# Wide attention: an earlier first norm, SyncE for the first transfers, maxima spread over the batches, and halves swapped by ScalarE

## The chip, the cores and the metric

The kernel runs on one core of one Trainium2 chip. Time is device microseconds from start to end of one launch. A core has five engines with a queue of instructions each: TensorE (PE; its weight loads are shown as PEld), VectorE (DVE), ScalarE (ACT), GpSimd (POOL) and SyncE (SP, which only starts transfers). ScalarE, SyncE and POOL can issue DMAs. An engine works through its queue in order; engines wait for each other through semaphores, which the Tile framework places from the data that instructions share.

## What is computed

x has 8 batches of 512 rows of 128. Two sublayers follow one another, each as x + layernorm(f(layernorm(x))):

```
x = x + ln(attention(ln(x)))      # one head of width 128, rope, causal; q, k, v and output weights 128x128
x = x + ln(ffn(ln(x)))            # ffn(x) is itself two steps:
    h = rmsnorm(x, g1) @ w_down                     # 128 -> 64
    a = x + attention16(h @ wq, h @ wk, h @ wv) @ w_up   # 16 heads of width 4, rope, causal
    t = rmsnorm(a, g2)
    f = a + sum over the 2 best of 8 experts of gate * (silu(t @ w1[e]) * (t @ w3[e])) @ w2[e]
ln(x) = (x - mean) / sqrt(var + 1e-5);   rope: (even, odd) -> (even*cos - odd*sin, even*sin + odd*cos)
```

In the wide attention "even" and "odd" are the first and the second 64 of the 128 columns.

## The kernel before

All of x, the running result (`h_all`) and all weights stay in SBUF. The work has three stages.

**Wide attention** (class `Wide`, driven by `wide_attention`). One batch is four row tiles of 128. Per batch: statistics of x (`stats_x`, VectorE and POOL), normalised rows on ScalarE (`norm`, L297), four transposes on TensorE and one copy (`turn`), projections to q and k with the rope (`project`), the scores with a causal mask added by a matmul (`scores`, L343 and L344), the maximum of each row on VectorE (L349) and the exponential on ScalarE (L351, which also yields the row sums), transposes of the probabilities (`turn_probs`, L367) and their copies to SBUF, the values (`values`, with `wvo`, the product of value and output weights), the weighted sum (`weigh`, L380), and later the closing: norm of the result (`norm_result`, `add_result`), its sum with x (`add`) and the statistics of that sum (`norm_sum`). The loop is a software pipeline written out by hand: in the round of batch b, batch b+1 is normalised and turned, b is projected and scored, b-1 has its probabilities turned and weighed, and b-2 is closed. Each round has four steps, at whose ends the generator yields.

For the rope the weights of q and k lie in SBUF twice, as they are and with their halves exchanged (`wqk`, six loads). `project` is called twice per batch; each call makes two 128x512 matmuls, multiplies the pair by the cosine and sine tables in one VectorE operation of 1024 columns (L316), and adds the two halves on POOL (L318).

**Head attention** (`Unit`, `period`). A unit is four of the 16 heads of one batch; there are 32. `ffn_front` makes q and k of a batch, splits them into three bf16 parts and writes them to DRAM (L552); `load_rows` reads them back in another layout (L560); both run on POOL's queue. For each unit, `rowwise` and `highest` (L600, L615) find the maximum of each row, in six pieces; `lower` and `turn_m` put these maxima into rows of q, with six small SyncE loads (L641), and then `columnwise`, `weights` and `weigh` (L656, L679, L686) make the transposed scores, their exponentials and the weighted sums. `period(n)` has seven steps; it finds maxima for unit n+2 while it works on unit n. So periods -2 and -1 hold nothing but maxima of units 0 and 1 and the turning of the first.

**Experts** (`experts`, L849 to L874), batch by batch.

What runs beside what is written in the driving loops: at each yield of the wide attention one step is taken from a list of tasks (`setup`: weight preparation and fixed rows; `first`: the front of batch 0; `fronts`: that of batch 1; `then`: periods -2 and -1). In the periods, `aside` takes a step from the fronts of later batches or from the backs of earlier ones. Inside `tc.manual_schedule()` the order on each engine is the order of the program text. The loads ahead of it are outside.

PSUM has eight banks of 512 columns of float32: three tiles of two banks ("wide") and two single banks ("bank") in the first stage, which in the second become one single bank and one for the weighted sums ("po").

Of the kernel before, what the change touches and what calls it, by code (L numbers as in the profile page):

```python
# [22 lines left out]
def kernel(  # L23
# [58 lines left out]
    for b in range(B):  # L82
        nc.sync.dma_start(
            out=x_all[:, b * NT : (b + 1) * NT, :],
            in_=x[b].rearrange("(t p) d -> p t d", p=P),
        )


    wqk = const.tile([P, 2, 2, D], F32, name="wqk")
    for i, w in enumerate((a_wq, a_wk)):  # L90
        nc.scalar.dma_start(out=wqk[:, i, 0, :], in_=w[0])
        nc.scalar.dma_start(out=wqk[:, i, 1, 0 : D // 2], in_=w[0][:, D // 2 : D])
        nc.scalar.dma_start(out=wqk[:, i, 1, D // 2 : D], in_=w[0][:, 0 : D // 2])
    ropea = const.tile([P, 2, T], F32, name="ropea")
    nc.scalar.dma_start(out=ropea, in_=rope_a)
# [5 lines left out]
    wdown = const.tile([P, L], F32, name="wdown")  # L101
    nc.gpsimd.dma_start(out=wdown, in_=w_down)
    wqkv = const.tile([L, 3, L], F32, name="wqkv")
    for i, w in enumerate((f_wq, f_wk, f_wv)):
        nc.gpsimd.dma_start(out=wqkv[:, i, :], in_=w)
    wup = const.tile([L, D], F32, name="wup")
    nc.gpsimd.dma_start(out=wup, in_=w_up)
    wr = const.tile([P, E], F32, name="wr")
    nc.gpsimd.dma_start(out=wr, in_=router_w)
    g1c = const.tile([P, 1], F32, name="g1c")  # L110
    nc.gpsimd.dma_start(out=g1c, in_=g1.rearrange("(p o) -> p o", o=1))
    g2c = const.tile([P, 1], F32, name="g2c")
    nc.gpsimd.dma_start(out=g2c, in_=g2.rearrange("(p o) -> p o", o=1))
    ropef = const.tile([P, NT, 2, HD], F32, name="ropef")
    nc.gpsimd.dma_start(out=ropef, in_=rope_f.rearrange("(t p) s d -> p t s d", p=P))
# [3 lines left out]
    for s in range(2):  # L119
# [10 lines left out]
    ident_bf = const.tile([P, P], BF16, name="ident_bf")  # L130
    nc.vector.tensor_copy(ident_bf, ident)

    mask_a = const.tile([P, P], BF16, name="mask_a")
    nc.gpsimd.memset(mask_a, 0.0)
    nc.gpsimd.affine_select(
        out=mask_a,
        in_=mask_a,
        compare_op=ALU.is_ge,
        fill=NEG_BF,
        base=0,  # L140
        pattern=[[-1, P]],
        channel_multiplier=1,
    )

    def half_masks(name, sign):


        m = const.tile([P, 2, P], BF16, name=name)
        nc.gpsimd.memset(m, 0.0)
        for i in range(2):  # L150
            for h in range(2):
                at = m[i * HR : (i + 1) * HR, h, :]
                nc.gpsimd.affine_select(
                    out=at,
                    in_=at,
                    compare_op=ALU.is_ge,
                    fill=NEG_BF,
                    base=sign * HR * h,
                    pattern=[[-sign, P]],
                    channel_multiplier=sign,  # L160
                )
        return m

    mask_q = half_masks("mask_q", -1)
    mask_k = half_masks("mask_k", 1)

    order = const.tile([P, E], F32, name="order")
    for e in range(E):
        nc.gpsimd.memset(order[:, e : e + 1], float(E - e))
# [47 lines left out]
    half = const.tile([P, 2 * GT], F32, name="half")  # L217
    nc.gpsimd.memset(half, -0.5)

# [38 lines left out]

    wvo = const.tile([P, D], F32, name="wvo")

    def fuse_projections():
        ps = bank("wvo_ps")
        nc.tensor.transpose(ps[:, :P], wv, ident)
        wvT = work.tile([P, D], F32, tag="sq", name="wvT", bufs=1)
        nc.scalar.copy(wvT, ps[:, :P])
        ps = bank("wvo_ps2")
        nc.tensor.matmul(ps[:, :P], wvT, wo, start=True, stop=True)
        nc.scalar.copy(wvo, ps[:, :P])
# [9 lines left out]
    def stats_x(batches):  # L278
        st = ln_stats(x_all, batches[0] * NT, "x", len(batches) * NT)
        for i, b in enumerate(batches):  # L280
            x_stats[b] = st[0][:, i * NT : (i + 1) * NT, :], st[1][:, i * NT : (i + 1) * NT]

    class Wide:
# [7 lines left out]
        def norm(self):  # L291
            b = self.b
            mv, rstd = x_stats.pop(b)
            shift = minus_product(mv[:, :, 0], rstd, "shift_x", f"shift_x_{b}")
# [15 lines left out]
        def project(self, i):  # L310
            b = self.b
            pq = wide(f"pq_{b}_{i}")
            for s in range(2):
                nc.tensor.matmul(pq[:, s, :], wqk[:, i, s, :], self.xnT, start=True, stop=True)
            two = deep.tile([P, 2, T], F32, tag="pk", name=f"two_{b}_{i}", bufs=5)
            nc.vector.tensor_tensor(two, pq, ropea, ALU.mult)  # L316
            r = work.tile([P, T], F32, tag=f"roped{i}", name=f"roped_{b}_{i}", bufs=1)
            nc.gpsimd.tensor_tensor(r, two[:, 0, :], two[:, 1, :], ALU.add)  # L318
            self.roped.append(r)
# [40 lines left out]
        def turn_probs(self, t):  # L360
            b = self.b
            n, at = (t + 1) * P, t * (t + 1) // 2 * P
            if t == 0:
                self.pT = work.tile([P, 10 * P], F32, tag="pT", name=f"pT_{b}", bufs=1)
            ps = bank(f"pT_ps_{b}_{t}")
            for j in range(t + 1):
                nc.tensor.transpose(  # L367
                    ps[:, j * P : (j + 1) * P], self.probs[t][:, j * P : (j + 1) * P], ident
                )
            if t < 2:  # L370
                nc.vector.tensor_copy(self.pT[:, at : at + n], ps[:, :n])
            else:
                nc.scalar.copy(self.pT[:, at : at + n], ps[:, :n])
# [22 lines left out]
        def norm_result(self):  # L396
            self.r = ln_stats(h_all, self.b * NT, "r")
            self.shift = minus_product(
                self.r[0][:, :, 0], self.r[1], "shift_r", f"shift_r_{self.b}"
            )  # L400

        def add_result(self):
            n0 = self.b * NT
            for t in range(NT):
                nc.scalar.activation(
                    h_all[:, n0 + t, :],
                    h_all[:, n0 + t, :],
                    AF.Identity,
                    bias=self.shift[:, t : t + 1],
                    scale=self.r[1][:, t : t + 1],  # L410
                )

        def add(self):
            nc.gpsimd.tensor_tensor(
                x_all[:, self.tiles, :], x_all[:, self.tiles, :], h_all[:, self.tiles, :], ALU.add
            )

        def norm_sum(self):
# [13 lines left out]
            h_scale[b] = kept  # L432

# [68 lines left out]

    def ffn_front(b):
# [43 lines left out]
        for r in range(3):  # L547
            for dst, src in (
# [3 lines left out]
                nc.gpsimd.dma_start(out=dst.rearrange("a d h t -> (d h) a t"), in_=src)  # L552
# [3 lines left out]
    def load_rows(b):  # L556
        for rows, src in zip((q_rows[b % 2], k_rows[b % 2]), made[b][0:2]):
            halves = src.rearrange("r a d (p i) t -> i (r a d) p t", i=2)
            for i in range(2):
                nc.gpsimd.dma_start(out=rows[i * HR : i * HR + S9], in_=halves[i])  # L560
# [414 lines left out]

    def wide_attention():
        batches = [Wide(b) for b in range(B)]
        for g in ([0], [1]):
            stats_x(g)
        batches[0].norm()  # L980
        batches[0].turn()
        fuse_projections()
        for b in range(B + 2):
            yield b
            u = batches[b] if b < B else None
            nxt = batches[b + 1] if b + 1 < B else None
            v = batches[b - 1] if 0 <= b - 1 < B else None
            w = batches[b - 2] if 0 <= b - 2 < B else None
            if nxt:
                nxt.norm()  # L990
            if w:
                w.norm_result()
            if u:
                u.project(0)
            if v:
                v.turn_probs(0)
                v.turn_probs(1)
            if u:
                u.project(1)
            yield b  # L1000
# [3 lines left out]
            if w:  # L1004
                w.add_result()
# [5 lines left out]
            yield b  # L1011
            if v:
                v.weigh()
            if b + 2 < B:
                stats_x([b + 2])
# [4 lines left out]
            yield b  # L1020
            if u:
                u.scores(1)
            yield b
# [5 lines left out]

    with tc.manual_schedule():  # L1030
        steps = wide_attention()
        setup = [prepare(), fill()]
        first = [front_and_rows(0)]
        then = [period(-2), period(-1)]
        fronts.append(front_and_rows(1))
        banks(ctx, wide=3)
        with ExitStack() as stage:
            banks(stage, bank=2)
            for b in steps:
                if b > B:  # L1040
                    break
                if b < 3:
                    step(setup)
                elif b < 6:
                    step(first)
                elif b < 7:
                    step(fronts)
                else:
                    step(fronts)
                    step(then)  # L1050
            while step(then):
                step(fronts)
    banks(ctx, bank=1, po=1)
    with tc.manual_schedule():
        for n in range(N + 1):
            for _ in period(n):
                next(steps, None)
                aside()
        for _ in experts(0):
# [79 lines left out]
```

## Time and profile before

| | us |
|---|---|
| median of 3 runs (821.34 to 822.37) | 822.21 |
| the profiled execution | 826.83 |
| its span, from first to last instruction | 825.0 |
| TensorE busy | 734.2 (89%) |
| VectorE busy | 479.0 (58%) |
| ScalarE busy | 334.9 (41%) |
| POOL busy | 310.2 (38%) |

The span divides at three marks in the trace: the first score matmul (25.14), the first weighing of the head attention (174.52) and the first expert (about 477). In the profile's lines, "out<-in" names what an instruction writes and reads, "x4" stands for four of them merged into one line, and brackets tell how long the engine sat idle before and what ended the wait. A row of digits gives tenths in 40 slices of the span, of about 20.6 us each. PEclk is the clock that TensorE was granted, as a share of full speed.

### The profile page before, as it was taken

The numbers are of one execution on the slowest core, as the hardware profiler recorded it, in microseconds if no ns is written. First come the engines' busy times: TensorE is split into PE (matmuls) and PEld (weight loads), VectorE is DVE, ScalarE is ACT, GpSimd is POOL, SyncE is SP. The second block draws the span as 40 slices with busy tenths as digits, with TensorE's granted clock in tenths as the row PEclk, the third lists the DMA queues.
The fourth block names the chain that finished last, engine by engine and source line by source line (L and its number), as shares of the span: only waits on it lengthen the run. The fifth ranks groups of instructions, "written<-read, shape, count | busy, mean of one in ns | idle before, by whom it ended". The sixth has DMA issues, their size and how long they took to land. (4 is left out here: it accounts for less than half of the span.)

```text
span 825.0 us, 15055 instructions
## 1 busy us (share of the span) xinstructions
PE 734.2 (89%) x5886; PEld 436.8 (53%) x5886; DVE 479.0 (58%) x1069; ACT 334.9 (41%) x532; POOL 310.2 (38%) x638
## 2 busy tenths in 40 slices
PE   2989687479999999989889899999999999999994
PEld 1646454334444445444444455666666666666663
DVE  1565557657766767686866035745454545454543
ACT  2454343155666656565656623222222222222220
POOL 5476876636666757676725130101010101010101
PEclk9999799669999999999999999999999999999998
DMA  9002120402221304040400000000000000000000
GB/s 287 20 14 71 58 58 1 116 2 61 60 72 49 101 19 118 3 117 4 118 3 3 2 1 0 14 1 14 0 14 1 14 0 14 1 14 0 14 1 13
DMA packets 25770, 30.37 MB, mean 37 GB/s; under 512 B 6372, under 2 KB 20932, under 8 KB 25700
## 3 DMA queue, kind: packets, MB, share of 16 engines
q0 software_dynamic: 6944, 19.03, 8.9%
q1 hardware_dynamic: 17460, 9.48, 3.9%
q8 instruction: 46, 0.75, 0.4%
q10 hardware_dynamic: 1296, 0.92, 0.4%
q14 instruction: 24, 0.20, 0.1%
HBM read 15.73 MB, written 11.53 MB: 33 GB/s over the span
## 5 line engine op out<-in xcount | busy, mean ns | idle before, releaser
L615 DVE TENSOR_REDUCE nm<-sm 128x2 f32<-128x1024 f32 (+2 forms) x192 | 194.3, 1044 | 45.0 <-PE sm L583 27.8
L679 ACT ACTIVATE pk<-sT 128x1024 f32<-128x1024 f32 x160 | 160.8, 1024 | 76.7 <-PE sT L583 76.6
L857 ACT ACTIVATE sil<-ph 128x512 f32<-128x512 f32 x128 | 76.4, 597 | 251.8 <-PE ph L849 230.3
L858 DVE TENSOR_TENSOR hid<-sil,ph 128x512 f32<-128x512 f32 x128 | 87.3, 687 | 124.2 <-ACT sil L857 124.2
L865 PEld LDWEIGHTS py<-w2s,hid 128*128 128x128 f32 x1024 | 124.2, 192 | 31.9 <-issue 27.4
L849 PE MATMUL ph<-tT_all,w1s 128*128 128x512 f32 x256 | 132.5, 600 | 0.0
L849 PE MATMUL ph<-tT_all,w3s 128*128 128x512 f32 x256 | 131.6, 596 | 0.0
L865 PE MATMUL py<-w2s,hid 128*128 128x128 f32 x1024 | 124.8, 275 | 1.9 <-DVE h_all L874 1.2
L224 POOL TENSOR_TENSOR root_o<-ve_o,half 128x4 f32<-128x4 f32 x8 | 8.2, 1020 | 310.0 <-DVE ve_o L241 310.0
L686 PE MATMUL po<-pk,vpad 128*32 128x512 f32 (+3 forms) x1024 | 98.5, 452 | 0.0
L874 DVE SCALAR_TENSOR_TENSOR h_all<-py,gate_all,h_all 128x128 f32<-128x128 f32 x256 | 72.0, 344 | 30.3 <-PE py L865 30.3
L600 PE MATMUL sm<-k_rows,q_rows 61*128 61x256 bf16 (+3 forms) x512 | 72.7, 310 | 12.3 <-DVE nm L615 7.3
L849 PEld LDWEIGHTS ph<-tT_all,w3s 128*128 128x128 f32 x256 | 49.1, 192 | 62.0 <-issue 62.0
L656 PE MATMUL sT<-q_rows,k_rows 64*128 64x384 bf16 (+3 forms) x512 | 65.4, 303 | 14.6 <-DVE nm L615 8.4
L849 PEld LDWEIGHTS ph<-tT_all,w1s 128*128 128x128 f32 x256 | 44.3, 193 | 31.9 <-issue 21.1
L600 PEld LDWEIGHTS <-q_rows 61*128 61x128 bf16 x512 | 23.8, 95 | 63.7 <-issue 60.4
L583 PE MATMUL sm<-ident_bf,mask_q 64*128 64x64 bf16 (+1 forms) x768 | 49.9, 202 | 0.0
L583 PEld LDWEIGHTS <-mask_q 64*128 64x128 bf16 x768 | 39.6, 98 | 12.8 <-issue 1.7
L583 PE MATMUL sT<-ident_bf,mask_k 64*128 64x128 bf16 (+1 forms) x640 | 43.8, 208 | 0.0
L656 PEld LDWEIGHTS <-k_rows 64*128 64x128 bf16 x512 | 26.3, 94 | 27.1 <-issue 25.8
L583 PEld LDWEIGHTS <-mask_k 64*128 64x128 bf16 x640 | 31.2, 95 | 12.0 <-issue 0.5
L438 POOL CAST m<-nm 128x16 bf16<-128x16 f32 x32 | 6.3, 198 | 73.1 <-DVE nm L615 73.1
(170 smaller groups left out, 879.1 us busy)
## 6 DMA issues: line engine op xcount, KB each, us to landing
q_dram<-thirds POOLq DMA_DIRECT2D x24, 192.0 KB, 3.2
k_dram<-thirds POOLq DMA_DIRECT2D x24, 192.0 KB, 3.7
q_rows<-q_dram POOLq DMA_DIRECT2D x16, 288.0 KB, 5.1
k_rows<-k_dram POOLq DMA_DIRECT2D x16, 288.0 KB, 6.3
q_rows<-m3T SPq DMA_DIRECT2D x192, 2.0 KB
x_all<-in_L_attn_x_dram SPq DMA_DIRECT2D x8, 256.0 KB
out_dram<-y SPq DMA_DIRECT2D x8, 256.0 KB
w1s<-in_L_ffn_w_dram SPq DMA_DIRECT2D x2, 512.0 KB
```

Source lines behind the costliest of these rows:

```text
L224: nc.gpsimd.tensor_tensor(y, x, half[:, :n], ALU.pow)
L583: nc.tensor.matmul(out[:, :, h * HR : (h + 1) * HR], which[at, h, :], ident_bf[at, at].unsqueeze(1).to_broadcast([HR, out.shape[1], HR]), ...
L600: nc.tensor.matmul(sc[:, i, c * n : (c + 1) * n], self.q[at, 2 * self.g + pair, t * P : n], self.k[at, 2 * self.g + pair, :n], start=(c == 0),
L615: nc.vector.tensor_reduce(self.nm[:, :, pairs[0] : pairs[0] + w, t], sc[:, :, : w * n].rearrange("p i (c n) -> p i c n", n=n), AX.X, ALU.m ...
L656: nc.tensor.matmul(sc[:, i, c : c + n], self.k[at, 2 * self.g + pair, j * P : (j + 1) * P], self.q[at, 2 * self.g + pair, j * P :], start= ...
L679: nc.scalar.activation(p[:, :, :c], sc[:, :, :c], AF.Exp, scale=HD**-0.5)
L686: nc.tensor.matmul(po[h * HP : (h + 1) * HP, j * P :], vpads[self.g][:, j, h, :], self.p[j, h // 2][:, h % 2, :], start=(self.g == 0 and j ...
L849: nc.tensor.matmul(ph[:, i, :], w[:, e, c * P : (c + 1) * P], tT_all[:, b, :], start=True, stop=True,)
L857: nc.scalar.activation(sil, ph[:, 0, :], AF.Silu)
L858: nc.vector.tensor_tensor(hid[:, c, :], sil, ph[:, 1, :], ALU.mult)
L865: nc.tensor.matmul(py[:, t * P : (t + 1) * P], hid[:, c, t * P : (t + 1) * P], w2s[:, e, c, :], start=(c == 0), stop=(c == FC - 1),)
L874: nc.vector.scalar_tensor_tensor(h_all[:, n, :], py[:, t * P : (t + 1) * P], gate_all[:, n, e : e + 1], h_all[:, n, :], ALU.mult, ALU.add,)
```

## The change

1. **First norm in front of loads.** Statistics of batches 0 and 1 and the norm of batch 0 stand ahead of POOL's nine small loads and of the masks in the program text. `stats_x` also makes the shift (`minus_product`).
2. **SyncE for first transfers.** The rope table is loaded by SyncE after x's first batch instead of by ScalarE. The writes of q and k and the row loads of batches 0 and 1 go to SyncE (`queue`), those of later batches stay on POOL.
3. **Halves swapped by ScalarE.** `wqk` is loaded once, by two loads. `project` makes q and k with one matmul each, into one PSUM tile; four ScalarE copies of 64 partitions put each half into the other's place, VectorE multiplies the unswapped part by the cosines; `rotate`, later in the same step, multiplies the swapped part by the sines and adds the two on POOL.
4. **Turned probabilities.** Tiles 0 and 1 share a bank and are copied at once; all these copies are ScalarE's.
5. **Closing.** The mean of each row is taken out of the product of value and output weights (`fuse_projections`), so the result needs only its scale; `add` multiplies by it and adds to x in one VectorE operation per tile. Only batches 0 to 2 are closed inside the wide attention; 3 to 7 are closed by `close`, one step after each period.
6. **Maxima distributed.** Periods -2 and -1 are stepped through within rounds 5 to 8 of the wide attention, and six steps of period 0 directly behind it. Per yield, two tasks' steps are taken instead of one; weight preparation and fixed rows are through after eight yields.

```diff
-    wqk = const.tile([P, 2, 2, D], F32, name="wqk")
+        if b == 0:
+            ropea = const.tile([P, 2, T], F32, name="ropea")
+            nc.sync.dma_start(out=ropea, in_=rope_a)
+    wqk = const.tile([P, 2, D], F32, name="wqk")
     for i, w in enumerate((a_wq, a_wk)):
-        nc.scalar.dma_start(out=wqk[:, i, 0, :], in_=w[0])
-        nc.scalar.dma_start(out=wqk[:, i, 1, 0 : D // 2], in_=w[0][:, D // 2 : D])
-        nc.scalar.dma_start(out=wqk[:, i, 1, D // 2 : D], in_=w[0][:, 0 : D // 2])
-    ropea = const.tile([P, 2, T], F32, name="ropea")
-    nc.scalar.dma_start(out=ropea, in_=rope_a)
+        nc.scalar.dma_start(out=wqk[:, i, :], in_=w[0])
...
-        nc.scalar.copy(wvo, ps[:, :P])
+        mean = stat.tile([P, 1], F32, tag="wvo_mean", name="wvo_mean", bufs=1)
+        nc.vector.tensor_reduce(mean, ps[:, :P], AX.X, ALU.add)
+        nc.vector.tensor_scalar(mean, mean, 1.0 / D, None, ALU.mult)
+        nc.vector.tensor_scalar(wvo, ps[:, :P], mean, None, ALU.subtract)
...
-        def project(self, i):
+        def project(self):
             b = self.b
-            pq = wide(f"pq_{b}_{i}")
-            for s in range(2):
-                nc.tensor.matmul(pq[:, s, :], wqk[:, i, s, :], self.xnT, start=True, stop=True)
-            two = deep.tile([P, 2, T], F32, tag="pk", name=f"two_{b}_{i}", bufs=5)
-            nc.vector.tensor_tensor(two, pq, ropea, ALU.mult)
-            r = work.tile([P, T], F32, tag=f"roped{i}", name=f"roped_{b}_{i}", bufs=1)
-            nc.gpsimd.tensor_tensor(r, two[:, 0, :], two[:, 1, :], ALU.add)
-            self.roped.append(r)
+            pq = wide(f"pq_{b}")
+            for i in range(2):
+                nc.tensor.matmul(pq[:, i, :], wqk[:, i, :], self.xnT, start=True, stop=True)
+            half = D // 2
+            both = deep.tile([P, 2, T], F32, tag="pk", name=f"swapped_{b}", bufs=5)
+            for i in range(2):
+                swapped = both[:, i, :]
+                for h in range(2):
+                    nc.scalar.copy(
+                        swapped[h * half : (h + 1) * half], pq[(1 - h) * half : (2 - h) * half, i]
+                    )
+                r = work.tile([P, T], F32, tag=f"roped{i}", name=f"roped_{b}_{i}", bufs=1)
+                nc.vector.tensor_tensor(r, pq[:, i, :], ropea[:, 0, :], ALU.mult)
+                self.roped.append((r, swapped))
+
+        def rotate(self):
+            for i, (r, swapped) in enumerate(self.roped):
+                nc.vector.tensor_tensor(swapped, swapped, ropea[:, 1, :], ALU.mult)
+                nc.gpsimd.tensor_tensor(r, r, swapped, ALU.add)
+                self.roped[i] = r
...
         def norm_result(self):
-            self.r = ln_stats(h_all, self.b * NT, "r")
-            self.shift = minus_product(
-                self.r[0][:, :, 0], self.r[1], "shift_r", f"shift_r_{self.b}"
-            )
+            self.r = ln_stats(h_all, self.b * NT, "r")[1]
...
+        def close(self):
+            self.norm_result()
+            yield
+            self.add()
+            yield
+            self.norm_sum()
+            yield
...
+    batches = [Wide(b) for b in range(B)]
+    with tc.manual_schedule():
+        stats_x(0)
+        batches[0].norm()
+        stats_x(1)
...
...
+    def queue(b):
+        return nc.sync if b < 2 else nc.gpsimd
...
-                nc.gpsimd.dma_start(out=dst.rearrange("a d h t -> (d h) a t"), in_=src)
+                queue(b).dma_start(out=dst.rearrange("a d h t -> (d h) a t"), in_=src)
...
-                nc.gpsimd.dma_start(out=rows[i * HR : i * HR + S9], in_=halves[i])
+                queue(b).dma_start(out=rows[i * HR : i * HR + S9], in_=halves[i])
...
     def wide_attention():
-        for b in range(B + 2):
-            yield b
+        for b in range(B + 1):
...
+            w = batches[b - 2] if 0 <= b - 2 < CLOSED else None
             if nxt:
                 nxt.norm()
+            if u:
+                u.project()
             if w:
                 w.norm_result()
-            if u:
-                u.project(0)
             if v:
-                v.turn_probs(0)
-                v.turn_probs(1)
+                v.turn_probs(0, 1)
             if u:
-                u.project(1)
-            yield b
+                u.rotate()
+            yield
+            if b == 0:
+                fuse_projections()
...
+    CLOSED = 3
+    units_begin = [period(-2), period(-1)]
+    begun = period(0)
...
+            batches[0].turn()
+            fronts.append(front_and_rows(1))
+            for i, _ in enumerate(wide_attention()):
+                b = i // 4
                 if b < 3:
                     step(setup)
+                    step(setup)
+                elif b < 5:
+                    step(first)
+                    step(first)
+                else:
+                    step(first)
                     step(fronts)
-                    step(then)
-            while step(then):
+                    if b > 5 or i % 4 > 1:
+                        step(units_begin)
+            for _ in range(6):
                 step(fronts)
+                step(units_begin) or next(begun)
+    closes = [batches[b].close() for b in range(CLOSED, B)]
...
         for n in range(N + 1):
-            for _ in period(n):
-                next(steps, None)
+            for _ in period(n) if n else begun:
                 aside()
+            step(closes)
```

## The prediction

> **What bounds the kernel now.** I read the time slices first, then the engines' busy times by stage, then one batch of the wide attention instruction by instruction, then the totals of waits. TensorE and its granted clock over the run:
>
> ```profile
> PE   2989687479999999989889899999999999999994
> ...
> PEclk9999799669999999999999999999999999999998
> ```
>
> TensorE is at nine tenths almost everywhere after 190 us; the holes, and the lowered clock, lie between 60 and 180 us. By stage (columns: window, length, busy us and instructions of PE, PEld, DVE, ACT, POOL, granted clock, DMA share, GB/s):
>
> ```profile
> core 0: us, PE busy (x) PEld busy (x) DVE busy (x) ACT busy (x) POOL busy (x), PEclk, DMA share, GB/s
> ...
> 25.14:136.35 111.21, 94.21 (x488) 63.20 (x489) 63.76 (x225) 52.36 (x138) 75.12 (x126) 0.92 0.14 38
> 136.35:174.52 38.17, 19.30 (x177) 12.81 (x175) 25.07 (x73) 10.21 (x23) 24.24 (x45) 0.68 0.25 63
> 174.52:477.00 302.48, 275.86 (x3653) 143.19 (x3652) 201.07 (x232) 185.23 (x224) 173.25 (x398) 0.98 0.20 50
> ```
>
> Below, "scores" is the start of the first score matmul of a batch (L343): 25.14, 38.37, 50.86, 66.55, 82.47, 103.55, 116.25, 136.35 us for batches 0 to 7. The first row is that stretch, 111.2 us. The second is the drain: 38.2 us until the first weighing of the head attention (L686, 174.52), TensorE half idle at clock 0.68. After it come 302 us of units and 348 us of experts, which the change leaves as they are except for what it moves into the units. So the change is decided before 175 us. A batch without other work, from scores to scores:
>
> ```profile
> 38.37 0.39 PE L343 MATMUL sc<-roped,roped 128*128 128x128 f32 x2
> ...
> 43.28 0.69 ACT L351 ACTIVATE p<-sc,nmax 128x512 f32<-128x512 f32 x1 [0.76 <-DVE nmax L349]
> ...
> 43.96 1.64 ACT L297 ACTIVATE xn<-x_all,shift_x,root_x 128x128 f32<-128x128 f32 x4
> ...
> 44.49 1.22 DVE L316 TENSOR_TENSOR two<-pq,ropea 128x1024 f32<-128x1024 f32 x1
> ...
> 46.05 0.96 PE L367 MATMUL pT_ps<-ident,p 128*128 128x128 f32 x7 [1.15 <-DVE pT L371]
> ...
> 46.66 0.97 ACT L373 COPY pT<-pT_ps 128x384 f32<-128x384 f32 x2 [1.07 <-PE pT_ps L367]
> ...
> 47.19 1.16 PE L324 MATMUL pv<-wvo,xnT 128*128 128x128 f32 x8 [0.18 <-ACT pT L373]
> ...
> 48.19 2.40 PE L380 MATMUL pr<-v,pT 128*128 128x128 f32 x20
> ...
> 50.86 0.39 PE L343 MATMUL sc<-roped,roped 128*128 128x128 f32 x2
> ```
>
> This is one chain over engines: scores, four exponentials (the last from 43.28, its sum read by 44.06), norm of the next batch (ScalarE, 1.64), rope product (VectorE), turned probabilities, their copies, weighing (L380), next scores: 12.5 us, of which the last exponential ends 5.7 after scores. TensorE is busy for all but about 1.5. Where batches are longer, two things show: POOL is late (q and k writes L552 held it from 91.00 to 94.9, so the norm waited 5.39), and TensorE runs at half clock:
>
> ```profile
> 44.51:47.92 3.41, 2.08 (x14) 1.46 (x14) 2.86 (x5) 2.34 (x6) 3.09 (x5) 1.00 0.00 0
> 58.16:61.57 3.41, 1.35 (x10) 1.04 (x10) 3.24 (x10) 2.50 (x7) 2.66 (x5) 1.00 0.24 63
> 61.57:64.98 3.41, 3.41 (x18) 3.41 (x17) 0.01 (x1) 2.14 (x6) 3.36 (x5) 0.50 0.35 118
> 88.88:92.29 3.41, 1.21 (x3) 0.19 (x1) 3.38 (x12) 0.78 (x2) 3.33 (x5) 1.00 0.00 0
> ```
>
> ```profile
> 62.88 3.40 PE L380 MATMUL pr<-v,pT 128*128 128x128 f32 x20
> ...
> 95.44 1.65 ACT L297 ACTIVATE xn<-x_all,shift_x,root_x 128x128 f32<-128x128 f32 x4 [5.39 <-POOL shift_x L273]
> ```
>
> Cut on the clock's own grid of 3.41 us, a window with 2.08 us of matmuls keeps the full clock, one with 1.35 or 1.21 is followed by half. Weighing then takes 3.40 (2.40 at full clock).
>
> **The change, part by part.**
> *Start.* The first norm begins at 13.35, behind POOL's loads and masks. Now POOL computes its root right after the statistics (end 5.42): root 1.03, two small products 0.42, two load issues between 1.13: norm at 8.1, turned by 10.9, the two projections 2.65 (half of the 5.31 of the eight at 17.16) by 13.6. The gain doesn't reach the scores whole. ScalarE next does the second norm (1.65), and four copies with waits (below) to 16.2; only then the copy of the down weights, which the order on TensorE puts ahead of the fused value weights. Their chain (two products, two copies, and a new mean of three VectorE operations, 0.28 + 0.17 + 0.28) ends at 20.2, values and turn at starting clock 2.6 more: scores at 22.8. POOL's sums are there at 20.3 (its loads and masks end at 17.6). From SyncE the rope table (512 KB) lies ahead of x's second batch; that delays the latter by some 2 us and nobody waits. Gain 2.3.
>
> *Projection.* Four matmuls go (two of each pair), 1.9 us of TensorE per batch. In exchange ScalarE copies four 64x512 halves out of PSUM (0.579 each, by the copy onT L722 of the same shape), VectorE makes four 512-wide products (0.69, as L858) for two of 1.22 (+0.3), and the small pT copies go from VectorE (0.61) to ScalarE (0.475). In ScalarE's new order the four copies stand after the norm and before the three pT copies; TensorE has two single banks, so the third turned tile waits for the first pT copy, and weighing for the third. The saved matmuls lie where TensorE waits anyway; the added copies lie on the chain.
>
> Do the copies run back to back? The instruction list says no: the third waits for VectorE's first product, the products wait for ScalarE. The Trainium skill, "PSUM — Partial Sum Buffer", section on bank collisions, lets two engines work side by side in different banks, and the two halves do lie in different banks: then the block would be 2.2 us. This case's trace shows the wait all the same between two banks of one tile:
>
> ```profile
> DVE nmax L349 <- ACT p L351: 11.3, 16, 1.1
> ```
>
> (sixteen times, the 256- and 512-wide maximum behind the exponential of the other half.) I take the row: 1.1 + 0.8 (product and hand-over) + 1.0 = 2.9. By the rule each batch would be 0.75 shorter, 5 us in all.
>
> From the last exponential's end E: norm to 1.65, copies to 4.6, first pT copy to 5.1, third tile turned (0.55), values and weighing to next scores 3.67 (47.19 to 50.86 above): E + 9.4 at full clock. POOL's path, two products and two sums of 1.27, ends at E + 8.7, with the result's root before it at E + 10.5; hidden while TensorE is later. VectorE's product of two SBUF operands beside POOL is not in the trace; between 0 and the 1.28 of the cast L131 beside POOL, I take 0.3 per batch.
>
> *Clock.* TensorE now has nothing from 5.6 after scores (projection, first two turned tiles) to E + 5.1, that is 5.2 us per batch. The Trainium skill, "TensorE: Matmul & The Clock Gate", Part 1, has the clock fall after an idle window of about 3.4 us on a free-running grid: an idle 5.2 holds a whole one in half of the batches. The rows above show a fall already below half a busy window, and return after one full window: it falls in every batch and stays low for 3.2 to 6.6 us after work resumes, which costs half of that, 1.6 to 3.0. I take 2.1; by the page it would be 1.1, 6 us less in all. A batch: 5.7 + 9.4 + 2.1 + 0.3, some 0.3 in hand-overs = 17.8, against 12.5.
>
> *Loads on SyncE.* q and k writes and row loads of batches 0 and 1 (20 issues of some 0.65) leave POOL for SyncE's queue, where only such loads wait: this removes the 5.39 in the batch of 21.1 (82.47 to 103.55), and the clock fall with it. Rows of batch 0 land some 13 after scores 4, first needed 19 after it.
>
> *Maxima distributed.* Twelve score pieces of the first two units move from the drain into batches 5 to 8; each costs VectorE 0.69 to 1.22. Between two exponentials it delays E; TensorE's part (0.6) mostly fills gaps. Closing of batches 3 to 7 (norm, add, statistics: 4.25 of VectorE) moves into 15 periods of units; for batches 0 to 2 it lies in VectorE's gap before weighing ends.
>
> *The sum*, as scores: batch 0 22.8; 1 at 42.3 (5.7 + 0.65 rope copy on VectorE + 1.1 two rope copies on ScalarE + 12.1); 2 at 60.1; 3 at 78.8 (0.9 for hT); 4 at 99.1 (2.5 for pqk between scores); 5 at 116.9; 6 at 139.6 (17.8, a maximum and hoisted statistics 2.0, hT copy 0.5, pqk and a piece on TensorE 2.4); 7 at 156.6 (no norm -1.65, no turn, shorter idle, one maximum). Drain: E at 6.5, then VectorE's ten maxima and the result bound it, 13: first weighing at 176.2, where it was 174.5, with the same units' maxima done: +1.7. A drain of 38 is 19.6 now; the batches take it all back.
>
> *Units.* A period without side work is 7.67 us; at its edge VectorE waits for TensorE:
>
> ```profile
> 196.52 1.23 DVE L615 TENSOR_REDUCE nm<-sm 128x2 f32<-128x1024 f32 x1 [1.34 <-PE sm L583]
> ```
>
> The closing pieces (about 1.4 each) stand at that edge. Routing puts 1.25 of VectorE there once (394.27 to 395.5) and that period is 7.79 instead of 7.67. Fifteen pieces at 0.12 to 0.3: +2.5; if the edge is no cover, 15 x 0.7 = 10. Sum: +4.2. On the profiled execution (826.8 around a span of 825.0) this gives 831; on the median shown, 822.2, it gives 826.
>
> **The rivals.**
> *ScalarE's block is absorbed* (not slower): if the clock holds and E + 9.4 is kept, a batch is 15.7; six batches less 2.1, the start unchanged: 176.2 - 13 = 163, so 814. For it: the page's rule, and pieces in batches 5 to 8 that partly fill the idle stretch. Against: the windows above. It decides at a batch of 17.1, where the +4.2 is gone.
> *The maxima don't fit in* (slower still): each of the twelve VectorE pieces lengthens the batch by its full 1.0, 5 more than I count, and the closings cost their 10: 826 + 5 + 8 = 839. For it: VectorE is already between all exponentials. Against: the 1.34 gap.
> *The loads weren't what stalled* (the change doesn't do what it says): rows late on SyncE by more than 6, so that TensorE waits in batch 5; some 836. POOL's 5.39 speaks against it.
>
> **How the numbers follow.** My forecast has 0.50, 818 to 833 on its own, for ±0.7 per batch; the absorbed block 0.33 (806 to 818); the two slower ones 0.17 (834 to 846). The range 810 to 842 leaves out a tenth at each end. Under 0.2% (1.6 us) is about what a measurement of this kernel can't tell from no change. Within the forecast 0.36 of 0.50 is slower, 0.10 same, 0.04 faster; so slower 0.53, same 0.10, faster 0.37.
>
> **What would show it.** Right: scores 15 to 19 us apart in batches 1 to 4; ScalarE's L266 in pairs with a wait for VectorE between; TensorE waiting 4 us or more before the third turned tile; PEclk at or below 0.8 through 30 to 150 us; first weighing at 172 to 181; plain unit periods still near 7.7. Wrong: scores under 16 us apart with full clock (then it is faster), or unit periods with closings over 8.4.

## The result, and the profile after

The changed kernel takes 842.4 us (median, 840.8 to 843.9) where the kernel before takes 822.3 beside it: a ratio of 1.024 (95% interval 1.021 to 1.027), slower. I had forecast 826, with a range of 810 to 842: the sign was the likeliest one, the size was 16 us too small. The profiled execution took 842.9 us, its span is 841.1.

Time slices of the changed kernel, TensorE and its granted clock, and below them the stages in the columns explained before:

```profile
PE   3774757888898888898989989999999999999994
...
PEclk9886878999999999999999989999999999999998
```

```profile
24.66:163.01 138.35, 93.70 (x489) 68.43 (x489) 71.47 (x203) 63.48 (x149) 58.44 (x86) 0.79 0.11 32
163.01:181.24 18.23, 13.95 (x141) 9.70 (x139) 13.16 (x17) 6.64 (x16) 1.12 (x6) 0.91 0.44 121
181.24:493.00 311.76, 277.12 (x3662) 144.81 (x3660) 222.38 (x340) 186.04 (x225) 186.92 (x418) 0.99 0.19 48
```

TensorE is now thin from the second to the seventh slice (4 to 7 tenths); before, the thinnest were the seventh to the ninth (7, 4 and 7). From the first scores to the last it is 138.4 us instead of 111.2 (clock 0.79 instead of 0.92), the drain is 18.2 instead of 38.2, the units some 312 instead of 302 (these two rows end some 3.7 behind the first expert matmul, which starts at 489.39, and before at 473.24). First weighing is at 181.24, 6.7 later than before; the units add 9, the experts nothing. "Scores" are at 24.66, 43.22, 59.99, 85.57, 104.30, 124.66, 146.74 and 163.01.

The batch from the second scores to the third, from the timeline of the changed kernel:

```profile
43.22 0.39 PE L301 MATMUL sc<-roped,roped 128*128 128x128 f32 x2
...
48.80 1.64 ACT L242 ACTIVATE xn<-x_all,shift_x,root_x 128x128 f32<-128x128 f32 x4
...
50.45 1.17 ACT L266 COPY swapped<-pq 64x512 f32<-64x512 f32 x2
...
51.71 0.69 DVE L270 TENSOR_TENSOR roped<-pq,ropea 128x512 f32<-128x512 f32 x1 [3.62 <-ACT swapped L266]
...
52.44 1.17 ACT L266 COPY swapped<-pq 64x512 f32<-64x512 f32 x2 [0.81 <-DVE roped L270]
...
53.63 0.86 ACT L330 COPY pT<-pT_ps 128x384 f32<-128x384 f32 x2
...
54.16 1.11 PE L327 MATMUL pT_ps<-ident,p 128*128 128x128 f32 x4 [5.80 <-ACT pT L330]
...
55.07 1.91 PE L282 MATMUL pv<-wvo,xnT 128*128 128x128 f32 x8
...
56.78 2.94 PE L337 MATMUL pr<-v,pT 128*128 128x128 f32 x20
...
57.13 2.54 POOL L276 TENSOR_TENSOR roped<-roped,swapped 128x512 f32<-128x512 f32 x2
...
57.19 3.16 DVE L360 SCALAR_TENSOR_TENSOR x_all<-h_all,root_r,x_all 128x128 f32<-128x128 f32 x4 [0.33 <-POOL root_r L166]
...
59.99 0.39 PE L301 MATMUL sc<-roped,roped 128*128 128x128 f32 x2
```

Here are the predicted steps: exponentials until 48.9, the norm, two pairs of copies with a wait of 0.81 for VectorE between them, the pT copies, TensorE idle for 5.80 and then at half clock until 57.91 (values 1.91, weighing 2.94, which were 1.16 and 2.40). POOL's sums end at 59.67, hardly before the next scores. And one thing that I had not counted: VectorE's sum L360, four rows of 128, takes 3.16 us beside POOL's sums.

### The profile page after: what moved, and what is told of

Same layout as the page of the kernel before. It is cut to its first block, busy times and chain, and to the rows that moved or that the text cites. A ratio compares the mean times of both kernels' runs of the same rounds, so it can differ in the third digit from the quotient of the medians.

```text
span 841.1 us, 15013 instructions
## 1 busy us (share of the span) xinstructions
PE 730.7 (87%) x5854; PEld 441.6 (53%) x5854; DVE 495.5 (59%) x1104; ACT 344.9 (41%) x539; POOL 286.8 (34%) x594
## 5 line engine op out<-in xcount | busy, mean ns | idle before, releaser
L683 PE MATMUL sT<-q_rows,k_rows 64*128 64x384 bf16 (+3 forms) x512 | 65.0, 299 | 18.0 <-DVE nm L642 13.9
L627 PE MATMUL sm<-k_rows,q_rows 61*128 61x256 bf16 (+3 forms) x512 | 70.8, 303 | 5.7 <-ACT pk L706 3.2
L876 PEld LDWEIGHTS ph<-tT_all,w1s 128*128 128x128 f32 x256 | 44.3, 193 | 31.9 <-issue 21.1
L327 PE MATMUL pT_ps<-ident,p 128*128 128x128 f32 x80 | 16.9, 338 | 41.9 <-ACT pT L330 37.2
```

The lines of the kernel that those rows point to most:

```text
L327: nc.tensor.transpose(ps[:, i * P : (i + 1) * P], self.probs[t][:, j * P : (j + 1) * P], ident)
L627: nc.tensor.matmul(sc[:, i, c * n : (c + 1) * n], self.q[at, 2 * self.g + pair, t * P : n], self.k[at, 2 * self.g + pair, :n], start=(c == 0),
L683: nc.tensor.matmul(sc[:, i, c : c + n], self.k[at, 2 * self.g + pair, j * P : (j + 1) * P], self.q[at, 2 * self.g + pair, j * P :], start= ...
L876: nc.tensor.matmul(ph[:, i, :], w[:, e, c * P : (c + 1) * P], tT_all[:, b, :], start=True, stop=True,)
```

## The experiments

All times are medians beside runs of the kernel before, which gave 822.4 to 823.5 in the four groups. "Batches" are the times from scores to scores. A single batch varies between executions: the first two of the changed kernel took 18.56 and 16.77, but 19.27 and 17.43 in run 3, whose program is the same up to there, and the third of the kernel before took 15.70 and, profiled again, 14.09. A difference of up to some 1.6 us in a single batch is therefore no result by itself, unless its lines show the cause.

**1. The change without the swap.**

```diff
-            pq = wide(f"pq_{b}")
...
-                        swapped[h * half : (h + 1) * half], pq[(1 - h) * half : (2 - h) * half, i]
...
+                pq = wide(f"pq_{b}_{i}")
+                for s in range(2):
+                    nc.tensor.matmul(pq[:, s, :], wqk[:, i, s, :], self.xnT, start=True, stop=True)
...
+                nc.vector.tensor_tensor(two, pq, ropea, ALU.mult)
```

> The changed kernel with the swap undone: four projections and one 1024-wide product for each of q and k, as before; everything else of the change stays. Theory 'the swap block is the cost': a batch loses its 5.3 us of 17.8, plain batches fall from 17-19 us to 12.5-14, first weighing from 181 to 150-156, time 842 to 810-818. Rival 'the closings and the maxima in the wide attention are the cost': batches 2 to 6 stay at 17 us and more, first weighing 170 or later, time 828-838.

(The loads of the exchanged halves are back too.) Measured: 805.9, ratio 0.979 (0.977 to 0.981), below what either theory gave. Batches 12.8, 11.7, 17.5, 13.9, 14.7, 17.1, 14.1; first weighing at 143.8. A batch of it:

```profile
36.52 0.39 PE L295 MATMUL sc<-roped,roped 128*128 128x128 f32 x2
...
42.11 1.64 ACT L244 ACTIVATE xn<-x_all,shift_x,root_x 128x128 f32<-128x128 f32 x4
...
44.16 0.65 PE L321 MATMUL pT_ps<-ident,p 128*128 128x128 f32 x4 [0.78 <-ACT pT L324]
...
45.55 2.44 PE L331 MATMUL pr<-v,pT 128*128 128x128 f32 x20
...
46.59 1.14 DVE L354 SCALAR_TENSOR_TENSOR x_all<-h_all,root_r,x_all 128x128 f32<-128x128 f32 x4 [1.15 <-POOL root_r L168]
...
48.26 0.39 PE L295 MATMUL sc<-roped,roped 128*128 128x128 f32 x2
```

TensorE waits 0.78 for the first pT copy instead of 5.80, and weighing has the full clock. The seven batches last 101.8 us against 138.4: the swap costs 36.6 there, 5.2 per batch in the mean (4.9 to 5.7 in five of them, 8.1 in the one of 25.58, 2.2 in the last). VectorE's sum takes 1.14, since POOL has done its sums by then.

**2. The swap alone, in the kernel before.** `project`, `rotate` and the single load of `wqk` as in the change, nothing else.

> The kernel before with the swap alone. Theory 'swap block': batches 1 to 7 each 4 to 5.5 us longer, less what POOL's waits in batches 4 and 5 already cost there: first weighing 174.5 to 195-205, time 822 to 845-855. Rival 'the block is absorbed where other work fills the batch': first weighing 174-180, time 822-828.

Measured: 860.7, ratio 1.046 (1.044 to 1.047), more than expected: the start is 2.4 later too. Batches 22.0, 18.8, 18.1, 20.4, 24.1, 20.6, 21.1. So the swap is worth +38 here and +36.5 in the changed kernel, and all the rest of the change -17: the parts add up to within 1 us.

**3. Closings without POOL's factors.**

```diff
+            if b >= CLOSED:
+                h_scale[b] = h_scale[0]
+                return
```

> The changed kernel; for the batches closed among the units (3 to 7) POOL's part of the last closing piece (the root of eight, two products, a negation; 2.3 us) is left out, and batch 0's factors stand in. VectorE's pieces stay. Theory 'POOL's part makes the hidden state late for the turn on TensorE': unit periods of 11.5, 11.9 and 10.6 us fall to 8.4-9.5, the one of 8.75 to 7.7; time 842 to 834-838. Rival 'VectorE's pieces at the period's edge are the cost': no period changes by more than 0.5, time 841-843.

Measured: 839.2. Between neighbouring copies of the turned maxima (L664), which I take as a period's length, 11.94 fell to 9.50, 8.75 to 7.80 and 8.65 to 8.38; 11.51 and 10.61 stayed. Of the three long periods that were to fall, one did. Right in kind, half in size: POOL's factors explain some 3.7 us, and what else delays the others had to be found in the trace (below).

**4. First turn of the hidden state one part later.**

```diff
+        if b == 0:
+            yield
         ps = transposed(hs, f"hT_ps_{b}")
```

> The changed kernel with the first batch's turn of the hidden state (hT) one part later in TensorE's order, behind weighing instead of ahead of it. Theory 'TensorE stands before it for POOL's hs': the batch of 25.6 us (scores 2 to 3) falls to 18.5-20 and most of it stays: time 836-839. Rival 'POOL is over-full there and the wait only moves': scores 4 moves by less than 2 us, time 841-843.

Measured: 838.3; the batch of 25.58 is 18.08, the next one 22.44 instead of 18.73. First weighing comes 5.2 earlier, the time is 4.1 less. The lines of the changed kernel that this removes:

```profile
76.04 2.52 POOL L276 TENSOR_TENSOR roped<-roped,swapped 128x512 f32<-128x512 f32 x2
...
78.56 1.89 POOL L472 TENSOR_SCALAR hs<-x_all,h_scale 128x128 f32<-128x128 f32 x4
...
79.19 1.79 PE L196 MATMUL hT_ps<-ident,hs 128*128 128x128 f32 x4 [3.29 <-POOL hs L472]
...
80.77 4.48 PE L337 MATMUL pr<-v,pT 128*128 128x128 f32 x20
```

The hidden state `hs` stands in POOL's order behind the two sums, TensorE's order has its turn ahead of weighing, and weighing, 3.3 us late, lies wholly in the half clock.

**5. Closings spaced.** The same pieces, but not after the one period in four at whose end POOL's squares begin.

```diff
-            step(closes)
+            if n % 4:
+                step(closes)
```

> The changed kernel; of every four unit periods, the one at whose end POOL's squares and sums of the result begin gets no closing piece, so that statistics, sum and factors fall on the other three. Same work. Theory 'what a closing costs is its place in POOL's order': the periods of 11.5, 11.9, 10.6 and 8.75 us fall to 8.4-9, at most 2 us come back where VectorE's sum meets POOL's split; time 842 to 834-838. Rival 'each piece costs wherever it stands': the cost moves, time 840-843.

Measured: 835.4, 7.0 less. The periods of 11.51, 11.94, 10.61 and 8.75 are 8.37, 8.37, 8.37 and 7.80; 9.46 is 8.19. Some of it comes back: two others are 12.16 and 10.28 where they were 10.82 and 9.83. In the changed kernel the worst of them reads:

```profile
265.60 1.67 POOL L387 TENSOR_TENSOR h_scale<-ve,half 128x8 f32<-128x8 f32 x1 [2.06 <-DVE ve L385]
...
268.02 1.03 POOL L770 TENSOR_TENSOR sq<-h_all 128x512 f32<-128x512 f32 x1
...
273.41 1.74 POOL L472 TENSOR_SCALAR hs<-x_all,h_scale 128x128 f32<-128x128 f32 x4
...
273.91 1.62 PE L196 MATMUL hT_ps<-ident,hs 128*128 128x128 f32 x4 [0.22 <-POOL hs L472]
...
275.96 1.23 DVE L642 TENSOR_REDUCE nm<-sm 128x2 f32<-128x1024 f32 x1 [2.04 <-PE sm L610]
```

POOL's squares `sq` start behind the factors (L387), so `hs` is late, the turn on TensorE waits for it piece by piece (1.62 instead of 0.66), and behind the turn stands the score that VectorE wants next (2.04). In the spaced version the same three steps are in time:

```profile
260.69 1.04 POOL L770 TENSOR_TENSOR sq<-h_all 128x512 f32<-128x512 f32 x1 [1.37 <-DVE h_all L757]
...
266.10 1.73 POOL L472 TENSOR_SCALAR hs<-x_all,h_scale 128x128 f32<-128x128 f32 x4
...
268.92 0.66 PE L196 MATMUL hT_ps<-ident,hs 128*128 128x128 f32 x4
```

**6. q and k in two PSUM tiles.**

```diff
-            pq = wide(f"pq_{b}")
+            pqs = [wide(f"pq_{b}_{i}") for i in range(2)]
```

> The changed kernel with q and k projected into two PSUM tiles instead of two banks of one tile. Theory 'ScalarE waits for VectorE because the tile is shared' (the row taken in the prediction): the third copy no longer waits 0.81 us, each of batches 1 to 7 is 0.5 to 0.75 shorter: time 842 to 837-839. Rival 'the products or POOL's sums end last and take the place of the wait': batches within 0.2 of the changed kernel's, time 841-843.

Measured: 834.4 (829.5 to 836.4), more gained than expected. The four copies run through:

```profile
49.87 2.37 ACT L266 COPY swapped<-pq 64x512 f32<-64x512 f32 x4
...
51.12 0.69 DVE L270 TENSOR_TENSOR roped<-pq,ropea 128x512 f32<-128x512 f32 x1 [3.62 <-ACT swapped L266]
...
52.25 0.86 ACT L330 COPY pT<-pT_ps 128x384 f32<-128x384 f32 x2
...
55.40 3.56 PE L337 MATMUL pr<-v,pT 128*128 128x128 f32 x20
...
59.23 0.39 PE L301 MATMUL sc<-roped,roped 128*128 128x128 f32 x2
```

The block is 2.37 instead of 3.16, so the wait came from the shared tile. Yet this batch is 16.60 instead of 16.77: the pT copies end 0.8 earlier after the scores, and weighing takes 3.56 instead of 2.94. The full clock came back at 57.84 here and at 57.91 in the changed kernel, so what resumed earlier ran at half clock for longer. Run 3 has the old block and a weighing as slow as this one, since its full clock came back only at 59.81:

```profile
43.74 0.39 PE L301 MATMUL sc<-roped,roped 128*128 128x128 f32 x2
...
52.95 1.17 ACT L266 COPY swapped<-pq 64x512 f32<-64x512 f32 x2 [0.81 <-DVE roped L270]
...
57.30 3.60 PE L337 MATMUL pr<-v,pT 128*128 128x128 f32 x20
...
61.17 0.39 PE L301 MATMUL sc<-roped,roped 128*128 128x128 f32 x2
```

That batch is 17.43, so at an equal clock the separate tiles are worth the 0.8 of the wait. Of the other batches four gain 1.0 to 2.1 and two gain 0.1 to 0.2. How much of that is the clock was not worked out, nor why the units are 3.1 longer in this profiled execution.

**7. Without the swap, first loads on POOL.** `queue` returns POOL for all batches.

> The changed kernel with the swap undone, and the q and k writes and row loads of batches 0 and 1 on POOL's queue again. Theory 'POOL's loads held the norm' (the prediction's step): the batches that hold them (scores 4 to 6) get 3 to 6 us longer in all, time 806 to 809-813. Rival 'the loads weren't what stalled': each batch within 1 us, time 805-808.

Measured: 808.6 (803.2 to 809.6), ratio 0.982 (0.978 to 0.985). The interval overlaps that of run 1, so the two are not told apart; no batch differs from run 1 by more than 0.8, and 1.5 of the difference of the profiled executions lie in the units.

**8. Without the swap, later turn, spaced closings** (edits 1, 4 and 5 together).

> The changed kernel with the swap undone, the first turn of the hidden state one part later and the closings spaced. If the three costs are separate: 806 less 4 less 6, that is 794-799. If the turn's delay was only the swap's (POOL's sums late) and the closings' cost is fixed: 802-806.

Measured: 794.9, ratio 0.967 (0.963 to 0.970). It beats both kernels. Edits 4 and 5 take 11.0 off the time of run 1, and took 4.1 and 7.0 off that of the changed kernel one by one: the three costs are separate.

**9. Filler turns to hold the clock.**

```diff
+            if 0 in tiles and b < 2:
+                for _ in range(16):
+                    nc.tensor.transpose(ps[:, n : n + P], self.probs[0][:, :P], ident)
```

> The changed kernel; in the batches after the first two, TensorE turns one tile sixteen times more (some 4.4 us of idle work into unused columns) behind the first two turned tiles, while ScalarE swaps. Theory 'half of what follows runs at half clock': the clock holds, turned tiles, values and weighing take their full-clock 0.65, 1.16 and 2.40 us, the batches of 18.56 and 16.77 us (scores 0 to 1, 1 to 2) become 16.6-17.2 and 14.9-15.3. Rival 'POOL's sums end last there anyway': both within 0.4 of the changed kernel's.

Measured: 842.3, batches 18.44 and 16.62. It decides nothing: the sixteen turns took 1.9 us, 4.05 stayed idle, and the clock fell.

**10 and 11. In the kernel before: SyncE's loads alone, and the norm's two products ahead alone.**

> The kernel before with the q and k writes and row loads of batches 0 and 1 on SyncE's queue alone. Theory 'POOL's writes held the norm' (the prediction's step): the wait of 5.39 us before the norm goes, the batch of 21.1 us falls to 15-16.5, time 822 to 815-819. Rival 'the wait returns elsewhere': 821-824.

> The kernel before with the norm's two small products on POOL made right behind the root (a batch earlier) alone; the writes stay on POOL. Theory 'the place of the two products decides, whatever queue the writes use': the wait of 5.39 us goes, the batch of 21.1 us falls to 15-16.5, time 822 to 815-819. Rival 'the queue decides': batch of 20-21, time 821-824.

Measured: 817.7, ratio 0.993 (0.991 to 0.995), 5.8 less, the batch of 21.1 at 16.2; and 824.6, ratio 1.002 (1.000 to 1.003). With the products ahead the norm no longer waits for the writes, but the closing's root does, and ScalarE's next operation for that:

```profile
95.69 0.63 POOL L552 DMA_DIRECT2D k_dram<-thirds  x1
...
96.34 1.06 POOL L224 TENSOR_TENSOR root_r<-ve_r,half 128x4 f32<-128x4 f32 x1
...
98.03 1.65 ACT L405 ACTIVATE h_all<-h_all,shift_r,root_r 128x128 f32<-128x128 f32 x4 [3.62 <-POOL shift_r L273]
```

The batch of 21.1 is 17.4, but the next one 17.3 where it was 12.7: the place of the products moves the wait, only the queue takes it away. In the changed kernel no ScalarE operation stands behind that root any more, which would explain why run 7 lost so little; no run tests that.

**12. The kernel before, profiled again.**

> The kernel before, once more with a profile: its own profiled execution was 826.8 us where the median is 822.2. If that is one slow stretch, it shows as one batch or unit period that is longer there than here; if it is spread, no single one differs by more than 1 us.

Its span is 820.2 where the first was 825.0: 1.1 less before first weighing, 2.8 in the units (1.57 of it in one period) and 0.9 in the experts, counted from the first expert matmul. Spread, not one place, though one period exceeds the 1 us expected.

**13 and 14. Longer fillers: in the changed kernel, and with two PSUM tiles** (36 and 32 turns).

> The changed kernel with thirty-six filler turns (4.6 us by the 0.129 of the last run) in the batches after the first two, so that TensorE is idle for about 1 us only. Theory 'the half clock sets the end' (the 2.1 of the prediction): clock 1.00 there, values and weighing 1.16 and 2.40 us, batch of 16.77 becomes 15.0-15.4. Rival 'POOL's two sums end 0.2 to 0.3 before the scores and take over': clock 1.00, but the batch stays at 16.3-16.8.

> q and k in two PSUM tiles, and thirty-two filler turns in the batches after the first two. Theory 'what the shorter block gained was eaten by a weighing wholly at half clock (3.56 us)': the batch of 16.60 (scores 1 to 2) becomes 15.5-15.9, bounded by POOL's sums. Rival 'no gain from the clock': it stays at 16.4-16.8.

Measured: 840.2 and 831.5; by their intervals the 2.2 of run 13 are not told from no change of the whole. In run 13 the clock held in the first of the two batches, and 18.56 became 16.50. In the second, which is the one that I had named, it fell all the same, and nothing was gained (16.79). In run 14 it held in both: 16.11 and 15.87, and the second ends so:

```profile
51.52 2.44 PE L340 MATMUL pr<-v,pT 128*128 128x128 f32 x20
...
53.09 2.54 POOL L276 TENSOR_TENSOR roped<-roped,swapped 128x512 f32<-128x512 f32 x2
...
55.68 0.49 PE L301 MATMUL sc<-roped,roped 128*128 128x128 f32 x2 [1.28 <-POOL roped L276]
```

Weighing ends at 53.96 and the scores then wait 1.28 for POOL's sums.

## Why the prediction was wrong

Two terms of the sum failed: the 0.9 for the turn of the hidden state, in a batch that came out 6.9 longer than forecast, and the +2.5 for the closings among the units, which came out at +9.4. Moving the turn took back 4.1 (run 4) and spacing the closings 7.0 (run 5), of the 16 by which the time was missed. The swap, which I had taken for the largest cost, came as forecast. Of the signs named for being wrong one came: periods with closings over 8.4.

**Swap block: right.** Predicted 5.3 per batch; against run 1 the two plain batches, 1 and 2, give 5.7 and 5.0. The mean of 5.2 over all seven meets the forecast more closely than its parts do. The wait between the pairs of copies came, as the row of the maxima suggested, and was 0.81 (0.8 in the working); the block was 3.2 with it (2.9) and 2.4 in separate tiles, where VectorE's product runs from 51.12 to 51.81 beside ScalarE's copies from the other bank, and these still take 0.58 each. So the rule of the Trainium skill, "PSUM — Partial Sum Buffer", section on bank collisions, holds for banks, and it is the shared tile that made the wait.

**Clock: right in size, with a floor that I named too weakly.** It fell in each of the seven batches, as predicted; holding it was worth 2.1 to 2.8 in run 13 (predicted 2.1), as that batch took 18.56 to 19.27 where the clock fell in it (the changed kernel and runs 3 to 5). One slip: half of 6.6 is 3.3, not 3.0; the 2.1 doesn't rest on it. But in a batch with a closing POOL's sums end just ahead of the scores, and run 14 gained only 0.73 by the clock before they took over. In the changed kernel they end 16.45 after the scores before, so the 15.7 of my absorbed block was not to be had; even with the shorter copies run 14 stops at 15.87.

**Batches 2 to 3: the first step that failed.** I gave the turn of the hidden state 0.9. The batch took 25.6 for 18.7, and 18.1 once the turn stood later; in the end it cost 4.1. I had placed its matmuls on TensorE, but not asked when POOL would deliver `hs`. All other batches were within 2.6 of the forecast, and first weighing 5.0 late. The start counts for 1.9 of it, 1.1 of that in the projections, which took 3.78, not 2.65: the norm began 5.0 earlier (8.32 for 13.35), the scores 0.5 instead of 2.3.

**Units: the second one.** Predicted +2.5, with 10 if the edge were no cover. The lengthened periods add 11.4 against the second profile of before. The working took only VectorE's part, 1.4 per piece, and that part was hidden: statistics after periods with a quiet POOL cost 0.0 (7.67 and 12.20 us, as before). So the +10 of the working for a bare edge was near the measured size for another reason, which is luck. What costs is the place: factors ahead of POOL's squares (11.94, run 3), the result's root, which waits at the head of POOL's queue for VectorE's statistics while the squares stand behind it (10.61), and VectorE's sum beside POOL's work (11.51, and 9.46, where the four sums take 3.52 beside POOL's split of q and k and TensorE waits 1.46 for the maximum behind them):

```profile
222.88 2.73 DVE L360 SCALAR_TENSOR_TENSOR x_all<-h_all,root_r,x_all 128x128 f32<-128x128 f32 x4
...
226.80 0.47 PE L683 MATMUL sT<-q_rows,k_rows 64*128 64x512 bf16 x2 [2.00 <-DVE nm L642]
...
252.52 1.13 DVE L360 SCALAR_TENSOR_TENSOR x_all<-h_all,root_r,x_all 128x128 f32<-128x128 f32 x4
```

The first line is four such sums, alone 1.13 in the third, and the second is TensorE waiting for the maximum behind them. The first cause is isolated by run 3; the other two are read from the trace, and run 5 shows only that all of them go with the place (its five groups of sums among the units take 1.13 or 1.14 each).

**Loads on SyncE: right for the kernel before** (5.8 by itself, run 10); in the changed one run 7 shows no loss that is clear of noise. The rival that loads were not what stalled falls for the kernel before.

**Maxima distributed: fit in.** Batches 4 to 7 took 20.4, 22.1 and 16.3 where 17.8, 22.7 and 17.0 were forecast; the drain was 18.2 (19.6). Of the rival "don't fit in" only the closings came true, at more than their bound. What the earlier norm, the closing's new form and the distributed maxima are each worth, inside the -17, no run shows.

**The base.** My +4.2 was added to 826.8 and to 822.2 alike. By the spans the miss is 11.9 (5.0 before first weighing, 7 in the units); the other 4 come from the profiled execution of before, which was 4.6 above the median, the one after only 0.5. A second profile of before would have shown first weighing at 173.4.

## What to carry to other kernels

When work is moved into another stage, place its parts on every engine's queue: here the operations that I costed were hidden, and the small ones on POOL, whose order is fixed, made a turn on TensorE late in two stages. An idle stretch that a new step opens on TensorE costs more than itself when it lowers the clock, but only down to the next chain's end, so work out that floor before giving the clock its full price. And try the parts one by one: 17 us of gain lay under 36 of loss.

## What the runs showed of the hardware

The clock fell after a window that was far from idle. In run 13 TensorE's longest gap in it was 2.04 us; two neighbouring stretches of the clock's grid (length, then busy us and instructions of PE, PEld, DVE, ACT and POOL, and the granted clock before the last two columns):

```profile
49.46:52.88 3.42, 1.38 (x13) 1.14 (x12) 1.93 (x6) 2.21 (x6) 0.00 (x0) 1.00 0.30 92
52.88:56.29 3.41, 3.41 (x18) 3.41 (x18) 3.05 (x10) 1.07 (x2) 2.55 (x3) 0.50 0.36 120
```

A window with 1.38 busy of 3.42 is followed by a whole one at 0.50. The Trainium skill, "TensorE: Matmul & The Clock Gate", Part 1, has the clock fall after at least one idle window of some 3.4 us; here one that was two fifths busy did it. These traces give no sharp limit in its place: in run 1 a window with 1.79 us busy (58.17 to 61.58) was followed by one at 0.50, and in run 6 one with 1.43 (64.66 to 68.07) by one at 1.00.

VectorE's sum of two SBUF operands took 1.13 us for four tiles alone, 3.16 beside POOL's sums. Nearly all of the excess lies in the first two, which started while POOL's two sums ran (57.13 to 59.67):

```profile
57.19 2.63 DVE L360 SCALAR_TENSOR_TENSOR x_all<-h_all,root_r,x_all 128x128 f32<-128x128 f32 x2 [0.33 <-POOL root_r L166]
```

The two behind them took 0.34 each. POOL pays as well: the root beside VectorE's products took 1.34 instead of 1.04. The Trainium skill, "SBUF — State Buffer", section "Who interferes with whom", says so for a VectorE operation with two SBUF inputs against a POOL operation that reads SBUF; I had priced it for the rope product, 0.3, and not for the sum. No run here took POOL's reads away alone; in run 1, where its two sums end before VectorE's begins, the four take 1.14.
